# A graph-network kernel: the search for edge blocks runs alone, and sixteen groups of keys and values can wait for positions instead of eleven

## The chip, the cores and the metric

The kernel runs on one core of one Trainium2 chip. The metric is device time in microseconds (us) of one launch, the median of three runs. The profile is one more execution, with its own time. The engines are TensorE (PE, and PEld for its weight loads), VectorE (DVE), ScalarE (ACT), GpSimd (POOL) and SyncE (SP), which here only issues DMAs.

## The reference, cut to what matters

6250 nodes with 128 features, 200000 edges sorted by destination, 16 node types, 32 edge types, 8 heads of 16. `typed_linear` multiplies each node by the matrix of its own type. Two such layers run one after the other, then a projection, a residual and a normalisation.

```python
k = typed_linear(x, ntype, Wk).reshape(n, H, HS)
q = typed_linear(x, ntype, Wq).reshape(n, H, HS)
v = typed_linear(x, ntype, Wv).reshape(n, H, HS)
kT = jnp.einsum('nhd,htdo->nhto', k, Watt)
vT = jnp.einsum('nhd,htdo->nhto', v, Wmsg)
kw = kT[src, :, etype]
m = vT[src, :, etype]
a = jnp.einsum('ehd,ehd->eh', kw, q[dst]) * pri[:, etype].T / SQRT_D
att = edge_softmax(a, dst, n)
msg = (m * att[:, :, None]).reshape(-1, H * HS)
hag = jax.ops.segment_sum(msg, dst, num_segments=n)
h = jax.nn.silu(typed_linear(hag, ntype, Wa))
```

## The kernel before

Nodes are cut into 49 tiles of 128 and, for the preparation, into 25 groups of two tiles (the last has one). The time has two parts: a preparation that ends when the table of the first layer stands in DRAM, and two layers whose work is gathering rows of such tables, one row for each of 128 edges at a time (L914, 1613 gathers a layer).

The preparation has three strands, which share the engines:

- **Typed products** (`first_typed`, `one_typed`, `typed`). For each group its rows are loaded and transposed; for each of 16 types DVE makes a masked copy `xm` (L427), and PE multiplies it by that type's key and value weights into one PSUM bank `kv` (L442, 32 products for a group, which run as two passes each). Four `xm` buffers are there, so mask t waits for the product of mask t-4. Then `kv` is copied to `kT` and `vT` (L451, L453), which have KEPT buffers each.
- **The search** (`prepare`). Where each node's edges begin is found in steps: the destinations are compared with the first of each of 512 blocks (POOL writes `cols` L527, DVE makes 40 `less` tiles at L532 in two buffers, PE counts them at L536); the block numbers `blk_i` (L542) index 50 gathers on POOL (L550, ten `part` tiles of five gathers, two buffers); DVE counts in each (L558, L560); the degrees order the nodes (`hot` L599, a scan at L618), which gives their positions (`place32` L508). Records of the nodes follow (L651 to L660), and later steps that only the layers need.
- **Tables** (`first_tables`, `table_rows`). They wait for positions, since each row carries its node's. For each tile 16 products (L475, as four groups of four that run side by side) go through five PSUM banks `tab`, are copied by ACT or DVE into four staging tiles `st` of half a tile each (L484), get the position column (L840, twice a tile), and are written out (L865, four DMAs of 1028 KB a tile).

The order of each engine's instructions is written by a planner: steps of the strands are started by rank and by the time that the planner expects their inputs, and each engine's queue then runs in that order. An instruction that waits holds up all behind it on its engine. Queues of PE, DVE and ACT thus interleave the three strands, and the real times decide who waits. `plan.run()` is called for the preparation twice: once up to the test whether the edges are sorted (here they are, so `sort_edges` is skipped at run time), and once for the rest; the layers have a plan of their own.

Of the kernel before, what the change touches and what calls it, by code (L numbers as in the profile page):

```python
# [31 lines left out]
F32 = mybir.dt.float32  # L32
# [6 lines left out]
P = 128  # L39
# [12 lines left out]
XM = 4  # L52
MARGIN = 8.0
AHEAD = 2
KEPT = 11
STAGES = 4
SPARE = 1.0
DRIFT = 15.0
# [150 lines left out]
def dve_us(n):  # L209
    return 0.15 + n / 960  # L210


def act_us(n):
    return 0.14 + n / 1200
# [18 lines left out]
def gnn_kernel(ctx: ExitStack, tc: tile.TileContext, x, src, dst, etype, ntype, Wk, Wq, Wv, Wa,  # L233
               Watt, Wmsg, pri, skip, ln_g, ln_b, ff_w, ff_b, out):
    nc = tc.nc
    N, D = x.shape
# [3 lines left out]
    NTILE = -(-N // P)  # L240
# [3 lines left out]
    EC = KB * BL  # L244
    EP = P * EC
# [21 lines left out]
    def dtile(name, shape, dt=F32):  # L267
        return dram.tile(shape, dt, tag=name, name=name)
# [9 lines left out]
    dsort = dtile("dsort", [NBLK, BL], I32)  # L278
    csort = dtile("csort", [NBLK + 1, BL], I32)

    def ctile(name, shape, dt=F32):
        return const.tile(shape, dt, tag=name, name=name)


    ident = ctile("ident", [P, P])
# [57 lines left out]
    edges, flagged = {}, When()  # L343
# [103 lines left out]
    def copied(pool, tag, acc, M, bufs, needs):  # L447
        us, e = yield ("ACT", "DVE"), (act_us(M), dve_us(M)), needs
        t = pool.tile([P, M], F32, tag=f"{tag}{M}", name=tag, bufs=bufs)
        if e == "ACT":  # L450
            nc.scalar.copy(t, acc[:, :M])  # L451
        else:
            nc.vector.tensor_copy(t, acc[:, :M])  # L453
        return t, us
# [36 lines left out]
    ps = early.enter_context(tc.tile_pool(name="ps", bufs=1, space=bass.MemoryType.PSUM))  # L491
    NC1 = NTILE + 1
    ov = ctile("ov", [P, NTILE, 2], I32)
    placed, known = When(), When()
    place32 = first.tile([P, NTILE], F32, tag="place32", name="place32")
    kinds_r = first.tile([P, RT], F32, tag="kinds_r", name="kinds_r")
    nc.gpsimd.iota(kinds_r, pattern=[[1, RT]], base=0, channel_multiplier=0, allow_small_or_imprecise_dtypes=True)
# [13 lines left out]
    def prepare():  # L511
        stage = ExitStack()
        sp = stage.enter_context(tc.tile_pool(name="search", bufs=2, side="right"))
# [9 lines left out]
        for t0 in range(0, NC1, CB):  # L523
            n = min(CB, NC1 - t0)
            us = yield "POOL", 1.5, ()
            cols = sp.tile([P, CB, P], F32, tag="cols", name="cols")
            nc.gpsimd.iota(cols, pattern=[[1, CB], [NTILE, P]], base=t0, channel_multiplier=0,  # L527
                           allow_small_or_imprecise_dtypes=True)
            for k in range(KB):
                us = yield "DVE", 0.5, [us]  # L530
# [3 lines left out]
                for t in range(n):  # L534
                    c = k * NC1 + t0 + t
                    nc.tensor.matmul(blk_ps[:, c : c + 1], less[:, t], ones_b[:, 0:1], start=True, stop=True)  # L536
        us = yield "DVE", 1.0, [got]
# [2 lines left out]
        nc.vector.tensor_scalar(blk, blk, -1.0, 0.0, op0=ALU.add, op1=ALU.max)  # L540
        blk_i = pp.tile([P, NC1], I32, tag="blk_i")
        nc.vector.tensor_copy(blk_i, blk)  # L542
        begin = pp.tile([P, NC1], F32, tag="begin")
        seen = [us]
        for t0 in range(0, NC1, CB):
            n = min(CB, NC1 - t0)
            us = yield "POOL", n * GATHER_US, [us, *seen[-2:][:1]]
# [24 lines left out]
        sp = stage.enter_context(tc.tile_pool(name="order", bufs=1, side="right"))  # L572
# [8 lines left out]
        us = yield "DVE", 0.6, ()  # L581
# [3 lines left out]
        us = yield "DVE", 0.2, ()  # L585
# [10 lines left out]
        BT = BINS * NTILE  # L596
# [4 lines left out]
        us = yield "DVE", 0.3, ()  # L601
# [3 lines left out]
        total = sp.tile([P, BT], F32, tag="total")  # L605
# [3 lines left out]
        for lhs, to in ((ones_b, total), (upper, ahead)):  # L609
            for c0 in range(0, BT, 448):  # L610
                us = yield "PE", Work(112), [counted]
                n_ps = tabs[c0 // 448 % len(tabs)]
                nc.tensor.matmul(n_ps[:, :448], lhs, hot_f[:, c0 : c0 + 448], start=True, stop=True)
                us = yield "ACT", act_us(448), [us]
                nc.scalar.copy(to[:, c0 : c0 + 448], n_ps[:, :448])
        yield "DVE", 2 * dve_us(BT), [us]
        upto = sp.tile([P, BT], F32, tag="upto")
        nc.vector.tensor_tensor_scan(upto, total, total, 0.0, op0=ALU.add, op1=ALU.max)  # L618
        yield "DVE", dve_us(BT), ()
        nc.vector.tensor_tensor(upto, upto, ahead, op=ALU.add)  # L620
# [2 lines left out]
        us = yield "DVE", dve_us(BT), ()  # L623
# [8 lines left out]
        us = yield "DVE", 1.0, ()  # L632
# [10 lines left out]
        us = yield "DVE", 1.0, ()  # L643
# [4 lines left out]
        for t in range(NTILE):  # L648
            us = yield "DVE", dve_us(P) + dve_us(4 * NTILE), spent[-3:][:1]
# [5 lines left out]
            us = yield "PE", Work(4 * NTILE), [us]  # L655
# [3 lines left out]
        us = yield "DVE", dve_us(4 * NTILE), [us]  # L659
# [5 lines left out]
        us = yield "DVE", 0.3, [us]  # L665
# [9 lines left out]
        for g in WIDE:  # L675
# [5 lines left out]
            for j, t in enumerate(g):  # L681
                us = yield "POOL", XG_US, ()
# [7 lines left out]
        for t in range(NTILE):  # L690
            span = slice(offset[t], offset[t] + profile[t])
            us = yield "POOL", GATHER_US, ()
# [16 lines left out]
        us = yield "DVE", 0.8, ()  # L709
# [4 lines left out]
        us = yield "PE", Work(P), [us]  # L714
# [9 lines left out]
        for g in WIDE:  # L724
            n = len(g)
            us = yield "DVE", dve_us(n * P), ()
# [3 lines left out]
            us = yield "PE", Work(n * 32), [us]  # L730
# [3 lines left out]
            us = yield "ACT", act_us(n * P), [us]  # L734
# [8 lines left out]
        us = yield "DVE", dve_us(NTILE * NT), ()  # L743
        nc.vector.tensor_tensor(one_of, ty[:, :, None].to_broadcast([P, NTILE, NT]),
                                kinds[:, None, :].to_broadcast([P, NTILE, NT]), op=ALU.is_equal)
        for i in range(L):
            us = yield "SP", 0.4, ()
            sk = sq.tile([P, NT], F32, tag="sk", name=f"sk{i}")
            nc.sync.dma_start(out=sk, in_=skip[i][None, :].to_broadcast([P, NT]))
            us = yield "DVE", 2 * dve_us(NTILE * NT), [us + 3.0]  # L750
# [3 lines left out]
            us = yield "ACT", 1.6, [us]  # L754
            nc.scalar.activation(alpha[i], alpha[i], AF.Exp, scale=-1.0)
            us = yield "DVE", 1.0, [us]
# [15 lines left out]
    sts = [first.tile([P, RT // 2, ROW + 1], F32, tag=f"st{c}", name=f"st{c}") for c in range(STAGES)]  # L772
# [5 lines left out]
    def bank(pool, name):  # L778
        return pool.tile([P, GT * P], F32, tag=name, name=name)

    tabs, kv, xb = [bank(ps, f"tab{i}") for i in range(5)], bank(ps, "kv"), bank(ps, "xb")

    def load_nodes(n0, n):
        t = ap.tile([P, GL, P], F32, tag="rows", name="rows", bufs=3)
        full = min(n, (N - n0) // P)
        if full < n:
            nc.vector.memset(t, 0.0)
        if full:
            nc.sync.dma_start(out=t[:, :full], in_=x[n0 : n0 + full * P].rearrange("(j p) d -> p j d", p=P))
        if full < n:  # L790
            left = N - n0 - full * P
            nc.sync.dma_start(out=t[:left, full], in_=x[n0 + full * P : N])
        return t
# [2 lines left out]

    def first_typed(part):
        for i in part:
            g = GROUPS[i]
            n0, n = g[0] * P, len(g)  # L800
            M = n * P
            got = yield "SP", 0.9, read[-3:][:1] if i > 2 else ()
            rows = load_nodes(n0, n)
            ti = ap.tile([P, HALF], I32, tag="types_i", name="types_i")
            valid = min(M, N - n0)
            if valid < M:
                nc.vector.memset(ti, -1)
            nc.sync.dma_start(out=ti[:, :valid], in_=ntype[n0 : n0 + valid][None, :].to_broadcast([P, valid]))
            plan.spawn(one_typed(i, rows, ti, got + 3.0), RANK["typed"])
            read.append(masked_at[i])  # L810

    masked_at = [When() for _ in GROUPS]
    def one_typed(i, rows, ti, got):
        g = GROUPS[i]
        n = len(g)
        M = n * P
        us = yield "DVE", dve_us(M), [got] + ([masked_at[i - 2]] if i > 1 else [])
        tf = ap.tile([P, HALF], F32, tag="types", name="types")
        nc.vector.tensor_copy(tf[:, :M], ti[:, :M])
        xT, us = yield from transposed(xb, rows, n, [got] + ([masked_at[i - 1]] if i else []))  # L820
        end, masked_at[i].us = yield from typed(
            ap, "xm", xT, tf, M, [(wk, kv[:, :HALF]), (wv, kv[:, HALF:])], [], [kv], (1,),
            made[i - 1] if i else 0.0, [us])
        if i >= KEPT:
            yield "SP", 0.0, [used[i - KEPT]]
        kT, ks = yield from copied(ap, "kT", kv[:, :HALF], M, KEPT, [end])
        vT, vs = yield from copied(ap, "vT", kv[:, HALF:], M, KEPT, [end])
        columns[i] = kT, vT
        made[i].us = max(ks, vs)
# [47 lines left out]
    with tc.manual_schedule():  # L877
        plan.spawn(first_typed(range(AHEAD)), RANK["typed"])
        plan.spawn(load_edges(), RANK["prepare"], 1.0)
        plan.spawn(relation_blocks(), RANK["late"], 25.0)  # L880
        plan.run()
    unsorted = nc.values_load(edges["flag"][0:1, 0:1], min_val=0, max_val=E)
    with tc.If(unsorted > 0):
        sort_edges(tc, ident, edges["dst_i"], edges["comb"], dsort, csort, EC, NTILE, N, EP, tabs)
        nc.sync.dma_start(out=edges["dst_i"], in_=dsort_rows)
    nc.vector.tensor_copy(bounds, edges["dst_i"].rearrange("p (k b) -> p k b", k=KB)[:, :, 0])
    prep.close()
# [1 line left out]
    with tc.manual_schedule():  # L889
        plan.spawn(first_typed(range(AHEAD, len(GROUPS))), RANK["typed"])  # L890
        plan.spawn(first_tables(range(len(GROUPS))), RANK["table"])
        plan.spawn(prepare(), RANK["prepare"], flagged.us + 6.0)
        plan.spawn(first_states(), RANK["late"])
        plan.run()
# [4 lines left out]
    tabs, ak, av = [bank(ps, f"tab{i}") for i in range(4)], bank(ps, "ak"), bank(ps, "av")  # L899
# [464 lines left out]
                plan.run()  # L1364


def sort_edges(tc, ident, dst_i, comb, dsort, csort, EC, NTILE, N, EP, banks):

    nc = tc.nc
    with tc.tile_pool(name="cnt", bufs=1, side="right") as cp:  # L1370
        psums = dict(t_ps=banks[0][:, :P], s_ps=banks[1][:, :NTILE], d_ps=banks[2][:, :P], n_ps=banks[3][:, :NTILE])

        def tl(name, cols, dt=F32):
            return cp.tile([P, cols], dt, tag=name, name=name)

        lanes = tl("lanes", P)
        nc.gpsimd.iota(lanes, pattern=[[1, P]], base=0, channel_multiplier=0,
                       allow_small_or_imprecise_dtypes=True)
        part = tl("part", 1)
        nc.gpsimd.iota(part, pattern=[[1, 1]], base=0, channel_multiplier=1,  # L1380
                       allow_small_or_imprecise_dtypes=True)
        lower = tl("lower", P)
        nc.vector.tensor_scalar(lower, lanes, part, None, op0=ALU.is_lt)
        upper = tl("upper", P)
# [110 lines left out]
```

## Time and profile before

| what | value |
|---|---|
| median of three runs | 5319.89 us (5318.32 to 5320.77) |
| the profiled execution, its own time | 5318.69 us |
| span, first to last instruction | 5316.9 us |
| preparation, up to the first layer's first gather | 865.51 us |
| busy: PE, DVE, ACT, POOL | 48%, 74%, 18%, 65% of the span |
| granted TensorE clock, mean | 0.690 of full |

The span is 1.8 us shorter than the execution's own time. The shares are means over stages with different limits: POOL gathers in the layers, while the preparation is a matter of PE, DVE and DMA. The rows further down cut the preparation into stages.

### The profile page before, as it was taken

Reading aid. Unit: us, or ns where it says so; the run is one execution under the profiler, and the core shown is the slowest. Engines: PE = TensorE matmul, PEld = TensorE weight load, DVE = VectorE, ACT = ScalarE, POOL = GpSimd, SP = SyncE. Lnnn points to the kernel's source line nnn. Section 1 sums busy time; section 2 is a strip of 40 time slices with the busy share of each in tenths; the row PEclk is TensorE's granted clock in tenths of the full one; section 3 lists DMA queues with packets and bytes.
Section 4 is the critical chain, followed back from the end, with each engine's and each line's share of the span. In section 5 each row is a group of like instructions: output and inputs, shape, how many; then the busy total and the mean of one; then the engine's idle time right before and its main releaser. Section 6 shows DMA issues by size and latency. Waiting matters only on the chain. (4 is left out here: it accounts for less than half of the span.)

```text
span 5316.9 us, 36038 instructions
## 1 busy us (share of the span) xinstructions
PE 2575.6 (48%) x8599; PEld 1371.0 (26%) x8599; DVE 3924.0 (74%) x5652; ACT 930.8 (18%) x1917; POOL 3451.2 (65%) x3446
## 2 busy tenths in 40 slices
PE   6799994036646665676668731213223321221113
PEld 5555452013223332333234510101101111110002
DVE  5766663688887887778888727777777777776777
ACT  0133441002212222222224310000000000000001
POOL 2214103677777777777777347777777777777775
PEclk8899996567866676667778865656656655655556
DMA  3399898336556556665667544333333333333332
GB/s 98 113 354 396 340 374 269 97 104 235 158 184 232 176 170 226 233 203 180 206 220 286 222 148 121 102 115 115 116 106 114 115 110 105 110 112 108 110 103 74
DMA packets 324030, 925.54 MB, mean 174 GB/s; under 512 B 83047, under 2 KB 170132, under 8 KB 286176
## 3 DMA queue, kind: packets, MB, share of 16 engines
q0 software_dynamic: 162752, 441.12, 28.2%
q1 hardware_dynamic: 161056, 482.05, 24.2%
q8 instruction: 68, 1.11, 0.1%
q14 instruction: 154, 1.26, 0.1%
HBM read 489.36 MB, written 433.57 MB: 174 GB/s over the span
## 5 line engine op out<-in xcount | busy, mean ns | idle before, releaser
L914 POOL DMA_INDIRECT ring<-table,idx_all x3226 | 3230.5, 1001 | 1421.0 <-issue 1079.5
L938 DVE TENSOR_TENSOR ring<-ring,sb 128x2048 f32<-128x2048 f32 (+13 forms) x261 | 453.9, 1739 | 664.8 <-DMA ring<-table,idx_all 646.6
L969 DVE TENSOR_REDUCE add<-ring 128x128 f32<-128x2048 f32 (+13 forms) x269 | 749.5, 2786 | 7.8
L484 ACT COPY st<-tab 128x512 f32<-128x512 f32 x1138 | 601.3, 597 | 574.0 <-PE tab L475 454.5
L1048 DVE SCALAR_TENSOR_TENSOR xm<-types,xb 128x512 f32<-128x512 f32 (+3 forms) x880 | 486.7, 589 | 93.5 <-PE av L1056 79.0
L475 PE MATMUL tab<-bv,vT 32*128 32x512 f32 x1568 | 429.5, 804 | 113.1 <-ACT st L484 108.5
L940 DVE TENSOR_REDUCE sb<-ring 128x128 f32<-128x2048 f32 (+13 forms) x269 | 472.9, 1758 | 6.8
L965 DVE TENSOR_TENSOR ring<-ring,sb 128x2048 f32<-128x2048 f32 (+13 forms) x269 | 469.5, 1745 | 0.0
L475 PE MATMUL tab<-bk,kT 32*128 32x512 f32 x1568 | 408.9, 788 | 71.9 <-ACT st L484 56.2
L1056 PE MATMUL tab<-xm,wq 128*128 128x512 f32 (+3 forms) x416 | 213.6, 680 | 465.3 <-DVE xm L1048 465.3
L484 DVE COPY st<-tab 128x512 f32<-128x512 f32 x430 | 280.1, 686 | 210.5 <-PE tab L475 167.7
L1056 PE MATMUL av<-xm,wa 128*128 128x512 f32 (+3 forms) x736 | 323.2, 599 | 203.1 <-DVE xm L1048 202.5
L1056 PE MATMUL av<-xm,wq 128*128 128x512 f32 (+3 forms) x544 | 239.4, 593 | 129.1 <-DVE xm L1048 127.2
L1210 ACT COPY sb<-qr 128x128 f32<-128x128 f32 x96 | 25.9, 270 | 1556.2 <-DVE sb L940 1391.9
L442 PE MATMUL kv<-xm,wk 128*128 128x256 f32 (+1 forms) x800 | 266.5, 417 | 38.8 <-DVE xm L427 38.6
L442 PE MATMUL kv<-xm,wv 128*128 128x256 f32 (+1 forms) x800 | 249.3, 395 | 0.0
L1056 PEld LDWEIGHTS av<-xm,wa 128*128 128x128 f32 x736 | 152.2, 223 | 371.4 <-DVE xm L1048 248.8
L1056 PEld LDWEIGHTS tab<-xm,wq 128*128 128x128 f32 x416 | 100.3, 268 | 567.2 <-DVE xm L1048 507.5
L1056 PE MATMUL ak<-xm,wk 128*128 128x512 f32 (+3 forms) x480 | 228.4, 560 | 33.3 <-DVE xm L1048 33.3
L475 PEld LDWEIGHTS tab<-bv,vT 32*128 32x128 f32 x1568 | 177.2, 223 | 259.9 <-ACT st L484 203.7
L1056 PE MATMUL av<-xm,wv 128*128 128x512 f32 (+3 forms) x480 | 221.7, 546 | 0.0
L475 PEld LDWEIGHTS tab<-bk,kT 32*128 32x128 f32 x1568 | 166.6, 220 | 197.1 <-ACT st L484 114.4
(211 smaller groups left out, 2833.1 us busy)
## 6 DMA issues: line engine op xcount, KB each, us to landing
table<-st SPq DMA_DIRECT2D x196, 1028.0 KB
table<-st SPq DMA_DIRECT2D x98, 2048.0 KB
ring<-table,idx_all POOLq DMA_INDIRECT x3226
state<-init SPq DMA_DIRECT2D x2, 3528.0 KB
state<-state SPq DMA_DIRECT2D x98, 72.0 KB
types<-tyrow SPq DMA_DIRECT2D x20, 256.0 KB
rows<-in_x_dram SPq DMA_DIRECT2D x24, 128.0 KB
types_i<-in_node_type_dram SPq DMA_DIRECT2D x24, 128.0 KB
```

The source lines that it names most:

```text
L442: nc.tensor.matmul(to, w[:, t], xm, start=False, stop=last_of)
L475: nc.tensor.matmul(tab, cT[here, nodes], blk[here, t0 : t0 + per].rearrange("p t o -> p (t o)"), start=True, stop=True)
L484: (nc.scalar.copy if e == "ACT" else nc.vector.tensor_copy)(to, tab.rearrange("p (t o) -> p t o", o=width))
L914: nc.gpsimd.indirect_dma_start(out=ring[:, place], out_offset=None, in_=tables[layer], in_offset=bass.IndirectOffsetOnAxis(ap=idx[:, s : s ...
L938: nc.vector.tensor_tensor(kk, kk, q[:, None, :].to_broadcast([P, m, P]), op=ALU.mult)
L940: nc.vector.tensor_reduce(sc[:, s0 : s0 + m], kk.rearrange("p s (h d) -> p s h d", h=H), axis=AX.X, op=ALU.add)
L965: nc.vector.tensor_tensor(vv.rearrange("p s (h d) -> p s h d", h=H), vv.rearrange("p s (h d) -> p s h d", h=H), sc[:, s0 : s0 + m, :, None ...
L969: nc.vector.tensor_reduce(add, vv.rearrange("p s c -> p c s"), axis=AX.X, op=ALU.add)
L1048: nc.vector.scalar_tensor_tensor(xm[:, :M], types[:, :M], float(t), xT[:, :M], op0=ALU.is_equal, op1=ALU.mult)
L1056: nc.tensor.matmul(to[:, :M], w[:, t], xm[:, :M], start=(t == 0), stop=(t == NT - 1))
L1210: nc.scalar.copy(q, rows[0][:, j])
```

## The change

Three things change. The typed products from group AHEAD = 2 on are planned only after the search's blocks are known (`searched`). KEPT is 16 instead of 11. To find room for five more `kT` and `vT` buffers, the scan is done in place (`upto` is `total`), and the tiles of the sort that isn't run here lie in a staging tile. The first line of `first_typed`'s loop is the one that moves instructions.

```diff
-KEPT = 11
+KEPT = 16
...
-    placed, known = When(), When()
+    placed, known, searched = When(), When(), When()
...
         nc.vector.tensor_copy(blk_i, blk)
+        searched.us = us
...
-        upto = sp.tile([P, BT], F32, tag="upto")
+        upto = total
...
     def first_typed(part):
         for i in part:
+            if i == AHEAD:
+                yield "SP", 0.0, [searched]
             g = GROUPS[i]
...
-        sort_edges(tc, ident, edges["dst_i"], edges["comb"], dsort, csort, EC, NTILE, N, EP, tabs)
+        sort_edges(tc, ident, edges["dst_i"], edges["comb"], dsort, csort, EC, NTILE, N, EP, tabs, sts[0])
...
         def tl(name, cols, dt=F32):
-            return cp.tile([P, cols], dt, tag=name, name=name)
+            if dt is not F32:
+                return cp.tile([P, cols], dt, tag=name, name=name)
+            if name not in parts:
+                c0 = sum(t.shape[-1] for t in parts.values())
+                parts[name] = flat[:, c0 : c0 + cols]
+            return parts[name]
```

**First place: DVE, from the first block comparison on.** Before, with `less` the comparisons, `xm` the masks of the typed products, and `pr`, `bk` weights that wait for a load:

```order
L520 MEMSET ones_b 128x128
L532 TENSOR_SCALAR less<-cols,bounds 128x640
L819 CAST types<-types_i 128x256
L532 TENSOR_SCALAR less<-cols,bounds 128x640
L329 TENSOR_SCALAR pr<-pr 128x32
L330 TENSOR_TENSOR bk<-bk,pr 128x1024
L453 COPY vT<-kv 128x256
L427 SCALAR_TENSOR_TENSOR xm<-types,xb 128x256 x16
L819 CAST types<-types_i 128x256
L532 TENSOR_SCALAR less<-cols,bounds 128x640
```

Now, at the same place:

```order
L520 MEMSET ones_b 128x128
L532 TENSOR_SCALAR less<-cols,bounds 128x640 x40
L539 TENSOR_REDUCE blk<-pb 128x50
L540 TENSOR_SCALAR blk<-blk 128x50
L542 CAST blk_i<-blk 128x50
```

The weights, the copy of the first group's values and the sixteen masks of the second group have moved behind the search; PE's queue has the second group's products behind all of L536 as well.

**Second place: DVE, from the block numbers to the counts.** Before (L558 and L560 are the count in one `part` tile):

```order
L542 CAST blk_i<-blk 128x50
L819 CAST types<-types_i 128x256
L453 COPY vT<-kv 128x256
L427 SCALAR_TENSOR_TENSOR xm<-types,xb 128x256 x12
L558 TENSOR_TENSOR lt<-part,nid 128x1955
L560 TENSOR_REDUCE begin<-lt 128x5
L427 SCALAR_TENSOR_TENSOR xm<-types,xb 128x256 x4
L558 TENSOR_TENSOR lt<-part,nid 128x1955
```

Now (the count has the lines L559 and L561):

```order
L330 TENSOR_TENSOR bk<-bk,pr 128x1024
L453 COPY vT<-kv 128x256
L427 SCALAR_TENSOR_TENSOR xm<-types,xb 128x256 x16
L822 CAST types<-types_i 128x256
L427 SCALAR_TENSOR_TENSOR xm<-types,xb 128x256
L453 COPY vT<-kv 128x256
L427 SCALAR_TENSOR_TENSOR xm<-types,xb 128x256 x4
L559 TENSOR_TENSOR lt<-part,nid 128x1955
L561 TENSOR_REDUCE begin<-lt 128x5
L427 SCALAR_TENSOR_TENSOR xm<-types,xb 128x256 x5
L559 TENSOR_TENSOR lt<-part,nid 128x1955
```

The first count now stands behind 21 masks and both groups' hand-overs, where it stood behind 12 masks.

**Third place: PE, where one group's typed products end and the next begin, late in the tables.** Before, at tables of the sixteenth group (`vT_3423` and `kT_3413` are an older group's copies):

```order
L475 MATMUL tab4_124<-bk_246,kT_3413 128x512
L414 MATMUL xb_126<-ident_72,rows_4031 128x128 x2
L475 MATMUL tab0_120<-bv_256,vT_3423 128x512
L475 MATMUL tab1_121<-bv_256,vT_3423 128x512
L475 MATMUL tab2_122<-bv_256,vT_3423 128x512
L475 MATMUL tab3_123<-bv_256,vT_3423 128x512
L436 LDWEIGHTS zeros_104
L436 MATMUL kv_125<-zeros_104 128x512
```

Now, at tables of the twentieth (`kT_4707` is the copy of the `kv` that the first row here finishes):

```order
L442 MATMUL kv_125<-xm_4671,wv_99 128x256
L414 MATMUL xb_126<-ident_72,rows_4391 128x128 x2
L475 MATMUL tab3_123<-bk_246,kT_4707 128x512
L475 MATMUL tab4_124<-bk_246,kT_4707 128x512
L475 MATMUL tab0_120<-bk_246,kT_4707 128x512
L475 MATMUL tab1_121<-bk_246,kT_4707 128x512
L436 LDWEIGHTS zeros_104
L436 MATMUL kv_125<-zeros_104 128x512
```

The table products now use keys whose copy was only just asked for. Counted over PE's whole queue: when the first table product stands, 7.25 groups of typed products stand ahead of it before and 5.81 now; the last typed product stands behind 41.25 tiles of tables before and 47 now. In the layers the rows of every engine are the same in both.

## Rows read from the trace of the kernel before

**Rows 1.** Stages: length; busy PE, PEld, DVE, ACT, POOL; clock, DMA shares; GB/s.
```profile
39.00:102.00 63.00, 42.68 (x330) 33.55 (x329) 36.70 (x82) 0.75 (x2) 6.93 (x11) 0.79 0.12 17
102.00:187.00 85.00, 57.84 (x211) 45.07 (x209) 63.30 (x79) 2.04 (x6) 62.60 (x53) 0.82 0.47 128
346.00:375.00 29.00, 16.15 (x61) 8.88 (x60) 8.94 (x21) 4.70 (x9) 0.00 (x0) 0.71 1.08 369
375.00:470.00 95.00, 95.00 (x508) 55.07 (x506) 65.75 (x146) 36.40 (x68) 32.53 (x33) 1.00 1.02 406
566.00:642.00 76.00, 66.34 (x304) 34.17 (x303) 48.19 (x106) 30.72 (x61) 0.00 (x0) 0.91 0.74 298
642.00:766.00 124.00, 124.00 (x688) 73.45 (x687) 86.67 (x197) 48.02 (x90) 0.00 (x0) 1.00 0.90 367
766.00:837.00 71.00, 66.44 (x248) 36.96 (x240) 41.96 (x79) 35.69 (x62) 0.00 (x0) 0.66 1.00 414
```

**Rows 2.** The same for POOL's gathers of the first layer, L914.
```profile
866.00:3090.00 2224.00, 1615.13 (x1613) 0.71 0.59 196
```

**Rows 3.** Timeline, search: start, length, instruction, idle before and its releaser.
```profile
41.00 0.95 DVE L532 TENSOR_SCALAR less<-cols,bounds 128x640 bf16<-128x640 f32 x1 [0.75 <-POOL cols L527]
...
51.90 0.18 DVE L329 TENSOR_SCALAR pr<-pr 128x32 f32<-128x32 f32 x1 [9.29 <-DMA pr<-in_L_gnn_pri_dram]
...
70.83 0.55 DVE L532 TENSOR_SCALAR less<-cols,bounds 128x640 bf16<-128x640 f32 x1 [3.03 <-PE pb L536]
...
95.98 3.75 DVE L532 TENSOR_SCALAR less<-cols,bounds 128x640 bf16<-128x640 f32 x7 [0.25 <-PE pb L536]
...
102.51 1.18 POOL L550 DMA_INDIRECT part<-dsort,blk_i  x1 [5.96 <-DVE types L819]
```

**Rows 4.** Timeline of DVE and POOL: the first count, eleventh gather, `hot`.
```profile
113.95 2.19 DVE L558 TENSOR_TENSOR lt<-part,nid 128x1955 bf16<-128x1955 int32 x1
...
117.31 1.00 POOL L550 DMA_INDIRECT part<-dsort,blk_i  x1 [0.30 <-issue]
...
187.07 3.43 DVE L599 TENSOR_TENSOR hot<-bin__1343,bins 128x3136 bf16<-128x3136 f32 x1
```

**Rows 5.** Timeline of PE and ACT: typed products of the second group.
```profile
54.11 1.17 PE L442 MATMUL kv<-xm,wk 128*128 128x256 f32 x2
...
59.52 0.59 PE L442 MATMUL kv<-xm,wv 128*128 128x256 f32 x2
...
70.51 0.37 ACT L451 COPY kT<-kv 128x256 f32<-128x256 f32 x1 [30.77 <-PE kv L442]
```

**Rows 6.** Timeline of PE: the first four table products and the record product behind them.
```profile
233.22 1.14 PE L475 MATMUL tab<-bk,kT 32*128 32x512 f32 x8
234.29 0.60 PE L657 MATMUL pb<-what,here 128*128 128x196 f32 x2
234.72 0.59 PE L442 MATMUL kv<-xm,wk 128*128 128x256 f32 x2
```

**Rows 7.** Busy time by stage for the typed products alone, L442.
```profile
375.00:470.00 95.00, 57.97 (x235) 42.02 (x233) 1.00 1.02 406
...
642.00:766.00 124.00, 73.84 (x330) 55.35 (x328) 1.00 0.90 367
```

**Rows 8.** Busy time by stage for the table products alone, L475.
```profile
375.00:470.00 95.00, 39.55 (x264) 12.43 (x264) 1.00 1.02 406
...
642.00:766.00 124.00, 52.85 (x344) 17.12 (x345) 1.00 0.90 367
```

**Rows 9.** Timeline: last tiles, next weights, the first layer's gather.
```profile
824.53 0.37 DVE L840 TENSOR_SCALAR st<-kinds_r,place 128x16 f32<-128x16 f32 x2
...
834.57 0.37 DVE L840 TENSOR_SCALAR st<-kinds_r,place 128x16 f32<-128x16 f32 x2
...
853.80 0.77 SPq L308 DMA_DIRECT2D wq<-in_L_gnn_Wq_dram  x1
...
865.51 1.01 POOL L914 DMA_INDIRECT ring<-table,idx_all  x1 [303.35 <-DVE low L995]
```

More of the change, by code (lines that the diff above doesn't have):

```diff
@@ L1364, in gnn_kernel, with sort_edges @@
                 plan.run()
-def sort_edges(tc, ident, dst_i, comb, dsort, csort, EC, NTILE, N, EP, banks):
+def sort_edges(tc, ident, dst_i, comb, dsort, csort, EC, NTILE, N, EP, banks, room):
     nc = tc.nc
@@ L1371, in sort_edges @@
         psums = dict(t_ps=banks[0][:, :P], s_ps=banks[1][:, :NTILE], d_ps=banks[2][:, :P], n_ps=banks[3][:, :NTILE])
+        flat, parts = room.rearrange("p t c -> p (t c)"), {}
         def tl(name, cols, dt=F32):
-            return cp.tile([P, cols], dt, tag=name, name=name)
+            if dt is not F32:
[4 more added lines that the diff above has]
+            return parts[name]
         lanes = tl("lanes", P)
```

## The prediction

> **What bounds the kernel now.** I read the stages first. From 866 us on POOL issues one gather after another: 1613 of them fill 1615 of the 2224 us of the first layer [rows 2], and the order of instructions in both layers is untouched, so I take everything behind the first gather (5316.9 - 865.5 = 4451.4 us) as fixed. The change can only move the end of the preparation, 865.5 us.
>
> In the preparation the tables are the long piece. From 375 to 470 us and from 642 to 766 us PE is busy all the time at the full clock of 2.4 GHz, while DMA stands at a share of 1.02 and 0.90; from 766 us on only tables are left, PE's mean clock is 0.66 of full, and DMA sets the pace at a share of 1.00 [rows 1]. Two tiles that follow each other there are 834.57 - 824.53 = 10.0 us apart [rows 9]. So the tables have two limits close together: PE while typed products run beside them, DMA when they don't. They cannot start before positions are known, which is the end of the search's chain.
>
> In that chain the first place to look is the comparisons. The first runs at 41.00 us; DVE is then stuck until 51.90 us behind weights whose load is late, and the third comparison comes at 70.83 us, released by PE, whose queue had the second group's typed products in front. Where no masks stand between them, seven comparisons take 3.75 us, 0.54 each. The first block gather starts at 102.51 us [rows 3].
>
> **The change, step by step.**
>
> *The search alone.* 40 comparisons at 0.54 are 21.4 us. With the first as slow as it was (0.95, POOL writing beside it) and 1.4 us for the last count and the block numbers, the first gather is due at 41.0 + 0.4 + 21.4 + 1.4 = 64.2, say 64.4 us: 38 us earlier. The cover of this is nothing: the stretch from 39 to 102 us had PE busy for 42.7 us with work that is not removed, only put behind [rows 1]. If the comparisons cost what the mixed rows show, at most 0.95 each, the end would be 81; I take the pace of the seven, which is the same work without masks.
>
> *What is late next.* The first count now waits on DVE behind 21 masks (second place). After the block numbers, DVE does the cast, `pr`, `bk` and the copy of values, some 2 us, to 66; then the second group's products run. Before they took from 54.11 to the copy at 70.51, 16.4 us, the first passes 1.06 to 1.17 a pair and later ones 0.59 [rows 5], that is at 1.2 and then at 2.4 GHz. So they end near 83, and the count, which needs four or five more masks and the first product of the third group, starts near 86. POOL has two `part` buffers: its eleventh gather must wait for this count to have read the first (2.2 us), so it goes at 88.3, 23.9 us after the first gather. Before it went 117.31 - 102.51 = 14.8 us after [rows 4]. That gives back 9 us. The remaining 40 gathers and their counts are POOL's pace, as before: `hot` starts at 187.07 - 38.1 + 9.1 = 158.1 us, 29 us earlier. From `hot` to the first table product it was 233.22 - 187.07 = 46.1 us [rows 4, 6]; the steps between are the same and the in-place scan does the same work, so the first table product comes at 204.2. The bounds of this step: if the second group's products find the full clock, the count comes some 3 us sooner; if they stay at the lower one to the end, 32 products at some 0.85 instead of 0.43 put it 11 us later.
>
> The Trainium skill speaks against this step: "TensorE: Matmul & The Clock Gate" (Part 1) says that idleness throttles the array to half its clock and that activity releases it, and a search of one-column products is near idle. By that alone the second group would start slow, as it did before after a wait; the rows show that it recovered after some 5 us, so the sum keeps the 16.4 us, and the rule's worst case is the 11 us of the bound.
>
> *Sixteen buffers.* In PE's order typed products lead the tables by at most 5.81 groups now, where it was 7.25. A lead that small never asks for the twelfth buffer, let alone the sixteenth: no wait goes, none comes, 0 us.
>
> *PE's ledger from the first table product to the last typed one.* Four table products that run side by side take 234.29 - 233.22 = 1.07 us [rows 6], so a tile takes 4.28. A group of typed products is 64 passes and a tile of tables 32 passes: from 375 to 470 us there are 235 and 264, so (95 - 8.25 x 4.28) / 3.67 = 16.3 us a group; from 642 to 766 us 330 and 344, so (124 - 10.75 x 4.28) / 5.16 = 15.1 [rows 7, 8]. I take 15.7. Before: 25 - 7.25 = 17.75 groups and 41.25 tiles, 279 + 177 = 455 us, in the 533 us from 233 to 766. The other 78 us are the stall at 346 to 375 us, where PE was busy for 16 of 29 us at a DMA share of 1.08, the thin stretch at 566 to 642 us [rows 1], and 49 record products at 0.43 [rows 6], 21 us. All this work is still there; I keep 78. Now: 19.19 groups and 47 tiles, 301 + 201 = 502 us.
>
> *New idle time of PE.* The first ten tiles now have only 2.13 groups beside them: per tile 4.28 + 3.3, and with the records some 2.4, which is 10.0, as much as DMA needs for a tile [rows 9]. Two limits that are equal never overlap fully: 0 to 1.5 us a tile, I take 7 us in all. In the last nine groups each table product stands right behind the copy that it needs (third place). A copy is 0.37 us [rows 5]; bounds 0 and, if the copy queues behind two more of `tab`, some 2 us; I take 0.4, 4 us in all.
>
> *The sum.* 204.2 + 502 + 78 + 7 + 4 = 795 us for the last typed product, which was at 766. But then 7.75 tiles followed at DMA's pace, and now two: 8.6 us by PE, 20 by DMA; I take 14, so the last tile is numbered at 809 instead of 834.57. From there to the next weights' load it was 853.80 - 834.57 = 19.2 us [rows 9], with DMA behind; with less behind it 10 to 19, I take 16. That load comes at 825 instead of 853.8: 29 us less. The profiled execution, 5318.7, becomes 5290; the median lies 1.2 above it, so 5291.
>
> **The rivals.**
>
> *Handed back.* The 29 us of the chain are spent in the tables: a group costs 16.3 and not 15.7 (1.44 groups more, and 19.19 times 0.6: 11.5 us), and the second group's products stay at 1.2 GHz (11 us). Then 6 us are left: 5313. For it: PE is full in the rows already, and the work put behind was done under the search for nothing. Against it: the tail wasted PE for six tiles.
>
> *The stalls shrink.* The 78 us are not a law: 76 us at 566 to 642 had only 128 typed passes' worth of work, and with tables further ahead and fewer products at once the state writes may cost less. If 28 of the 78 go, it is 5263. Against it: DMA has 49 tiles of 10.0 us, so it can't end before 214 + 490 + 19 = 723 plus state writes and rows, some 40; 763 would be 90 us less, which bounds it.
>
> *Slower.* The hand-over in the third place: where the lead is one group, every table group waits for its `kT`, which ACT does in order behind copies that wait for a free staging tile, which waits for DMA. It decides from (29 + 10.6) / 9 = 4.4 us above my 0.4 for each of nine groups. At 6 us it would be 5291 + 9 x 5.6 = 5341. Against it: typed products of the same group stood between in the order, so that the last copies of `tab` are 1.9 us old when the key copy is asked for.
>
> *It doesn't do what it says.* The comparisons stay at the mixed pace since POOL and not PE held them; then the chain gains 20 instead of 38, and the end 11: 5308. I count it with the first rival.
>
> **How the numbers follow.** A measurement of this kernel tells some 0.2% (10.6 us) from no change. My forecast, 11 to 45 us less, 0.63. Stalls that shrink, 45 to 70 less, 0.13. Handed back, within 10.6 us, 0.18. Slower 0.06. Faster is then 0.76. The range takes in the bounds of the chain (-3, +11), of a group's price (15.1 to 16.3, 12 us each way) and of the tail (10 us each way), and reaches into the two neighbours: 5262 to 5318. The likeliest case's own is 5274 to 5308.
>
> **What the profile will show.** First gather near 64, eleventh 24 us behind it, `hot` near 158, first table product near 204. Ten tiles in the first 127 us of tables; the last typed product near 795; two or three tiles behind it; next weights near 825. Wrong would be: a first gather after 75, an eleventh gather without the pause, PE idle before table products whose `kT` is being copied, or a first layer whose length differs.

## The result, and the profile after

| | before | after |
|---|---|---|
| median of four runs each | 5320.33 us (5318.32 to 5321.04) | 5290.03 us (5288.56 to 5291.53) |
| the profiled execution, its own time | 5318.69 | 5290.87 |
| its span | 5316.9 | 5289.1 |
| the first layer's first gather | 865.51 | 836.64 |
| from there to the end of the span | 4451.4 | 4452.5 |

The ratio is 0.9944, with an interval of 0.9932 to 0.9957: 30 us faster, where 5291 us was forecast. In the profile the preparation ends 28.9 us earlier, and the layers have the length that they had.

The timeline of after shows the steps. They answer to [rows 3] (first comparison, first block gather), [rows 5] (copy of the second group's keys), [rows 4] (first count, eleventh gather, `hot`), [rows 6] (first table product) and [rows 9] (last tiles, next weights, first gather of the layers). Columns are as there.

```profile
40.48 23.39 DVE L532 TENSOR_SCALAR less<-cols,bounds 128x640 bf16<-128x640 f32 x40 [0.74 <-POOL cols L527]
...
65.36 1.18 POOL L551 DMA_INDIRECT part<-dsort,blk_i  x1 [4.69 <-DVE types L822]
...
83.62 0.37 ACT L451 COPY kT<-kv 128x256 f32<-128x256 f32 x1 [44.40 <-PE kv L442]
...
86.26 2.19 DVE L559 TENSOR_TENSOR lt<-part,nid 128x1955 bf16<-128x1955 int32 x1
...
88.72 1.00 POOL L551 DMA_INDIRECT part<-dsort,blk_i  x1 [10.44 <-DVE lt L559]
...
159.73 3.42 DVE L600 TENSOR_TENSOR hot<-bin__1197,bins 128x3136 bf16<-128x3136 f32 x1
...
207.88 1.14 PE L475 MATMUL tab<-bk,kT 32*128 32x512 f32 x8
...
345.26 1.57 ACT L484 COPY st<-tab 128x512 f32<-128x512 f32 x3 [23.56 <-DMA table<-st]
...
794.78 0.27 ACT L451 COPY kT<-kv 128x128 f32<-128x128 f32 x1 [0.92 <-PE kv L442]
...
806.26 0.37 DVE L843 TENSOR_SCALAR st<-kinds_r,place 128x16 f32<-128x16 f32 x2
...
824.54 0.77 SPq L308 DMA_DIRECT2D wq<-in_L_gnn_Wq_dram  x1
...
836.64 1.01 POOL L917 DMA_INDIRECT ring<-table,idx_all  x1 [295.62 <-DVE low L998]
```

One row now holds all 40 comparisons. `hot` comes 27 us earlier, the first table product 25, the next weights 29. The stages of after, columns as in [rows 1]:

```profile
39.00:65.00 26.00, 11.62 (x201) 8.35 (x201) 24.23 (x45) 0.22 (x1) 9.23 (x11) 0.60 0.22 24
...
208.00:307.00 99.00, 98.89 (x538) 55.21 (x541) 84.33 (x216) 45.26 (x86) 5.85 (x7) 1.00 0.91 374
307.00:366.00 59.00, 39.51 (x190) 22.83 (x190) 25.88 (x59) 14.07 (x27) 4.66 (x6) 0.83 1.03 355
366.00:462.00 96.00, 95.52 (x496) 56.00 (x497) 65.05 (x144) 35.90 (x67) 33.48 (x34) 1.00 1.02 403
...
560.00:631.00 71.00, 65.61 (x315) 36.30 (x314) 46.07 (x101) 31.28 (x62) 0.00 (x0) 0.95 0.77 307
631.00:795.00 164.00, 162.19 (x905) 97.28 (x908) 111.26 (x253) 63.17 (x120) 0.00 (x0) 1.00 0.87 349
795.00:808.00 13.00, 12.02 (x64) 6.66 (x56) 11.05 (x21) 9.34 (x17) 0.00 (x0) 1.00 1.02 419
```

In the search PE has a mean clock of 0.60 of full and is busy for 11.62 of 26 us. From 208 to 794 us it is idle for 32.2 us, and 19.5 of them lie in the stretch around the state writes (307 to 366). And the stretch in which tables are alone at DMA's pace, 71 us in [rows 1], has shrunk to 13. The layers, read as in [rows 2], hold the same 1613 gathers in a window of the same length:

```profile
837.00:3061.00 2224.00, 1613.69 (x1613) 0.71 0.59 195
```

### The profile page after: what moved, and what is told of

Read it like the earlier page. It is cut to its first block, busy times and chain, and to the rows that moved or that the text cites. A ratio compares the mean times of both kernels' runs of the same rounds, so it can differ in the third digit from the quotient of the medians.

```text
span 5289.1 us, 36056 instructions
## 1 busy us (share of the span) xinstructions
PE 2550.8 (48%) x8591; PEld 1346.7 (25%) x8599; DVE 3921.5 (74%) x5650; ACT 930.1 (18%) x1919; POOL 3451.4 (65%) x3446
## 5 line engine op out<-in xcount | busy, mean ns | idle before, releaser
L475 PE MATMUL tab<-bv,vT 32*128 32x512 f32 x1568 | 393.7, 771 | 114.1 <-ACT st L484 110.0
L475 PE MATMUL tab<-bk,kT 32*128 32x512 f32 x1568 | 384.0, 768 | 70.5 <-ACT st L484 54.5
L442 PE MATMUL kv<-xm,wk 128*128 128x256 f32 (+1 forms) x800 | 262.1, 411 | 45.7 <-DVE xm L427 45.3
L442 PE MATMUL kv<-xm,wv 128*128 128x256 f32 (+1 forms) x800 | 244.3, 388 | 0.0
L475 PEld LDWEIGHTS tab<-bv,vT 32*128 32x128 f32 x1568 | 162.0, 215 | 253.6 <-ACT st L484 195.6
L475 PEld LDWEIGHTS tab<-bk,kT 32*128 32x128 f32 x1568 | 156.1, 214 | 188.4 <-ACT st L484 109.5
```

The lines of the kernel that those rows point to most:

```text
L442: nc.tensor.matmul(to, w[:, t], xm, start=False, stop=last_of)
L475: nc.tensor.matmul(tab, cT[here, nodes], blk[here, t0 : t0 + per].rearrange("p t o -> p (t o)"), start=True, stop=True)
```

## The experiments

Twelve runs of seven kernels. Beside the first eight (the first set: kept11, parts4, states_early, after_counts and each of these `_again`) the kernel before takes 6466 to 6469 us, beside the last four (the second set) 5322 to 5326, as above. The first set ran on chips 2 and 8 and the second on chips 2 and 11, so the number of the chip doesn't tell them apart, and what does isn't known. In the first set the trace of kept11 agrees with that of after up to some 460 us (first count 86.47, `hot` 159.74) and then shows waits for "remote", of which before and after have none (last section). For that set I go by marks, that is by the start times of the instructions listed above, and compare with kept11, which has the order of after row for row. A ratio is always to runs of the kernel before on the same chip.

**The buffers alone, from both sides** (kept11, kept11_again, kept16_only).

```diff
 # kept11: after with
-KEPT = 16
+KEPT = 11
 # kept16_only: after with
-            if i == AHEAD:
-                yield "SP", 0.0, [searched]
```

> The changed kernel with eleven buffers for keys and values instead of sixteen; the order of every engine's instructions is the same. My theory: the whole gain is the search, and the twelfth to sixteenth buffers are never asked for, since typed products lead the tables by 5.8 groups at most: 5290 us, within 2 of the changed kernel, first block gather at 65, first table product near 208, next weights near 825. Rival (the buffers carry part of the gain, because ACT or DVE would wait for an old buffer to be read): a wait of the kT and vT copies for PE appears and the time lies between 5295 and 5320.

> The same kernel as in kept11, because that run's chip was one on which the kernel before took 6469 us and engines waited for 'remote', which the trace of before never shows. My theory (the order of the changed kernel with eleven buffers is the changed kernel): 29 to 30 us below the kernel before, 5290 where that takes 5320. Rival (the five buffers carry part): 5295 to 5320, with waits of the kT and vT copies.

> The kernel before with sixteen buffers and all that makes room for them, without the wait for the search: the order of instructions is that of before. My theory (buffers, in-place scan and shared tiles are worth nothing): ratio 1.000 within 0.002, first block gather near 102.5, hot near 187, first table product near 233, next weights 29 us behind those of kept11 on the same chip. Rival (the buffers carry part of the gain): ratio 0.997 or less.

Measured: kept11 has 0.9965 (0.9940 to 0.9990) and again 0.9949 (0.9931 to 0.9967), where after had 0.9944; its first gather is at 65.30, its first table product at 206.56. The copies of keys and values wait as in after (ACT's for PE's products, 150.3 us in 20 waits beside 148.4 in 19), and none for an older buffer's reader. kept16_only has 0.9994 (0.9985 to 1.0003), a median of 5317.62 against 5321.88; its first table product is at 232.83. Its first gather and its next weights:

```profile
102.40 1.19 POOL L551 DMA_INDIRECT part<-dsort,blk_i  x1 [6.72 <-DVE types L820]
...
852.41 0.77 SPq L308 DMA_DIRECT2D wq<-in_L_gnn_Wq_dram  x1
```

All three are within 1.4 us of before. So sixteen buffers, the in-place scan and the shared room are worth nothing that can be measured; the wait for the search is the change. It moves two things out of the search's way at once, the weights whose load is late and the second group's masks and products [rows 3]. No run moves one without the other, so how much each is worth stays open.

**The pause before the eleventh gather** (parts4, parts4_again, parts3).

```diff
 # after with KEPT = 11, and bufs=4 (parts4) or bufs=3 (parts3)
-            part = sp.tile([P, CB, BL], I32, tag="part", name="part")
+            part = sp.tile([P, CB, BL], I32, tag="part", name="part", bufs=4)
```

> The changed kernel with eleven buffers of keys and values, and four part buffers for the block gathers instead of two; the order of instructions is the same, only POOL's eleventh gather no longer waits for the first count. My theory (the pause of 10.4 us before the eleventh gather is what was given back, and the chain up to the positions sets when tables start, so what the chain gains the end gains): no idle time before the eleventh gather, 1.8 to 2.3 us between gathers' starts at most, hot at 149 to 152 instead of 159.7, first table product 8 to 10 us earlier, 5281 us (5279 to 5284). Rival A (counts and masks on DVE, not gathers, set the pace behind the first count): hot at 156 to 160, 5287 to 5290. Rival B (the tables are held by PE's sum of work and an earlier start is handed back): hot near 150, but next weights still at 822 to 825, 5288 to 5290.

> The same kernel as in parts4. There the eleventh gather had no pause, but three waits of DVE's masks for 'remote', 3.1 to 3.8 us each, put the first count from 86.5 to 97.7 us, and hot came at 158.5. Two theories now. If that delay belonged to that chip: first count at 86 to 87, hot at 149 to 152, 5280 to 5284 us. If gathers that run on beside the second group's products delay them on any chip: first count at 94 to 98, hot at 157 to 159, 5288 to 5290.

> The changed kernel with eleven buffers of keys and values and three part buffers; the order of instructions is the same. POOL may issue 15 gathers before it waits for the first count, where four buffers let it issue 20 and the second group's products then stood still behind masks that waited for 'remote'. Theory A (that halt needs the longer unbroken run of gathers): first count at 86 to 88, hot at 152 to 156, next weights 4 to 7 us before those of kept11 (875.4 and 876.6 where it ran). Theory B (any gathers beyond the tenth hold up the second group's products there): first count at 90 to 98, hot at 157 to 160, weights at 874 to 877. The time itself can hardly tell 5 us.

parts4 has 0.9955 (0.9935 to 0.9976) and again 0.9958 (0.9942 to 0.9973), no better than kept11; weights at 875.52 and 875.19, where kept11 has 875.43 and 876.60. The pause before the eleventh gather went (one of 8.54 us came before the twenty-first), but in these runs another wait came. The timeline of parts4, DVE, at the end of the second group's masks:

```profile
82.06 0.42 DVE L427 SCALAR_TENSOR_TENSOR xm<-types,xb 128x256 f32<-128x256 f32 x1 [1.71 <-PE kv L442]
85.58 0.42 DVE L427 SCALAR_TENSOR_TENSOR xm<-types,xb 128x256 f32<-128x256 f32 x1 [3.11 <-remote]
89.78 0.42 DVE L427 SCALAR_TENSOR_TENSOR xm<-types,xb 128x256 f32<-128x256 f32 x1 [3.78 <-remote]
...
97.66 2.19 DVE L559 TENSOR_TENSOR lt<-part,nid 128x1955 bf16<-128x1955 int32 x1
```

POOL issued gathers without a break from 65.6 to 91.6 us, and the first count slid from 86.5 to 97.7 (97.2 in the second run), so that `hot` gained 1 to 3 us. None of the three theories of the first expectation had foreseen that. `hot`, at 158.47, does lie in rival A's range, but rival A has the time lost behind the first count, and here it is lost ahead of it. The second theory of the repeat describes it, for the first set. parts4 has no run in the second, so whether the halt belongs to the first set's conditions or to the run of 20 gathers stays open.

parts3, of the second set, has 0.9936 (0.9922 to 0.9949), 5285.60 us. Its timeline, from the first and sixteenth gather to the next weights:

```profile
65.44 1.18 POOL L551 DMA_INDIRECT part<-dsort,blk_i  x1 [4.70 <-DVE types L822]
...
88.93 1.00 POOL L551 DMA_INDIRECT part<-dsort,blk_i  x1 [4.06 <-DVE lt L559]
...
154.10 3.42 DVE L600 TENSOR_TENSOR hot<-bin__1197,bins 128x3136 bf16<-128x3136 f32 x1
...
818.46 0.77 SPq L308 DMA_DIRECT2D wq<-in_L_gnn_Wq_dram  x1
```

The pause is 4.06 instead of 10.44 us, 6.4 less; `hot` comes 5.6 us earlier than in after, the first table product (201.61) 6.3, the next weights 6.1. What the chain gains, the end gains, one to one. There is no halt behind these 15 gathers: the first count is at 86.47, as theory A has it. The intervals of the ratios of parts3 and after overlap, so that is read from the marks.

**The state writes** (states_early, states_early_again, both3).

```diff
 # states_early: after with; both3: also KEPT = 11 and part bufs=3
-            yield "SP", 5.5, [placed]
+            yield "SP", 5.5, [searched]
             nc.sync.dma_start(
                 out=state.rearrange("(t p) c -> p t c", p=P),
```

In the traces the rows of PE, DVE, ACT and POOL stand in the order of after, by line and tile name; on SP the two writes move ahead of the rows of the groups that are loaded after the search.

> The changed kernel with the two state writes (7 MB) issued when the block numbers are known instead of behind the eleventh tile's tables. My theory (part of the 78 us of stalls is the state write, in which PE was busy for only 39.5 of 59 us while tables waited for DMA; DMA is at a share of 0.4 from 65 to 102 us, so it is free there): the wait of 23.6 us at 345 goes, the first count stays at 86 to 88, and of PE's 19.5 idle us some 17 come back: 5273 us (5269 to 5277). Rival A (DMA's total sets the tables, not when it writes): the wait comes back as shorter ones, 5287 to 5291. Rival B (the writes get in the way of the block gathers and of rows for the typed products): first count or hot 10 to 18 us later, 5275 to 5290.

> The same kernel as in states_early. There the tables from 309 to 366 us kept PE busy for 56.6 of 57 us, and the next weights came 19.9 us earlier than in kept11, with hot 1.7 us later. My theory: the same 18 to 20 us here, 5271 us (5269 to 5274). Rival (with DMA fast, the lead is lost to DMA-paced tables further on, which the other chip's waits had hidden): 5275 to 5290.

> states_early with eleven buffers of keys and values and three part buffers. If the two gains add (state writes 20 to 23 us, a shorter pause 4 to 7), next weights come 25 to 30 us before those of kept11 on the same chip, at 846 to 851 if kept11's are 876, and the ratio is 0.990. If the state writes, which run from 65.6 to 81 us, hold up the extra gathers, weights at 852 to 857 as in states_early.

states_early has 0.9907 (0.9886 to 0.9929) and again 0.9905 (0.9882 to 0.9928), and its next weights come at 855.56 and 853.08, 19.9 and 23.5 us before those of kept11. both3 has 0.9892 (0.9877 to 0.9907), 5263.19 us: 59 us below the kernel before beside it, the best of all. Its stage of the former stall, and its next weights:

```profile
302.00:360.00 58.00, 57.68 (x307) 33.76 (x309) 41.33 (x92) 22.93 (x43) 11.71 (x12) 1.00 1.02 411
```

```profile
66.00 15.50 SPq L874 DMA_DIRECT2D state<-init  x2
...
797.95 0.77 SPq L308 DMA_DIRECT2D wq<-in_L_gnn_Wq_dram  x1
```

PE is busy for 57.68 of 58 us where it was for 39.51 of 59. The weights come 20.5 us before those of parts3 and 26.6 before those of after, so the two gains add. `hot` is at 154.41, 0.3 us behind parts3, and the first count at 86.78 instead of 86.47: the writes, now at 66 us, hold the chain up by next to nothing.

**The ledger, pushed the other way** (after_counts, three times).

```diff
-        searched.us = us
...
         yield "DVE", 0.0, [landed]
         yield from wait
+        searched.us = seen[-1]
         yield "DVE", 0.3, ()
```

> The changed kernel with the typed products from the third group on planned after the last count of the search instead of after the block numbers. In PE's order 3.25 groups of typed products stand ahead of the first table product instead of 5.81; the last typed product stands behind 47 tiles as before. My theory (from the first table product to the last typed one it is PE's ledger: 15.7 us a typed group, 4.28 a tile, 85 to 89 us besides): the first table product within 5 us of the changed kernel's 208, then 2.56 groups more beside the tables, so the last typed product at 830 to 836 instead of 795, 5325 to 5331 us. Rival (the tables are held by DMA at 10 us a tile, and typed products fit beside them): the last typed product moves by under 15 us, 5290 to 5305.

> The same kernel as in after_counts. There the first table product came at 200.0 us, 6.6 earlier than in kept11, and the next weights 22.9 us later. My theory (ledger of 15.7 us for each of 2.56 groups, less 7 to 8 us of the chain): last typed product at 825 to 830, 5320 to 5326 us. Rival (part of the typed work fits beside DMA-paced tables, as the other chip had it): 5308 to 5316.

> The same kernel as in after_counts, once more, for a chip on which the kernel before takes 5320 us. On the other chip the first table product came 6.6 and 9.3 us earlier than in kept11 and the next weights 22.9 and 20.2 us later, where the ledger (15.7 us for each of 2.56 groups that move beside the tables, less the chain's gain) asks for 31 to 34. My theory: with no halts for 'remote' it is the ledger, next weights at 850 to 859 instead of 824.5, 5315 to 5324 us, ratio 0.9990 to 1.0008. Rival (about 10 of the 40 us are hidden, since DMA and not PE holds some of the stretches): weights at 841 to 849, 5306 to 5314 us, ratio 0.9970 to 0.9988.

The ratios are 0.9981 (0.9956 to 1.0006), 0.9979 (0.9959 to 0.9999) and 0.9984 (0.9975 to 0.9993). In the third the first table product comes 8.3 us before that of after, the last tile is numbered at 827 us, and the next weights come 21.1 later:

```profile
199.54 1.14 PE L475 MATMUL tab<-bk,kT 32*128 32x512 f32 x8
...
845.60 0.78 SPq L308 DMA_DIRECT2D wq<-in_L_gnn_Wq_dram  x1
```

My 850 to 859 was wrong, and the rival's 841 to 849 holds; that the time, 5319.27, falls into my range is no support, since the kernel before took 5326.47 beside it, and the ratio is in the rival's range. So 2.56 groups beside the tables cost 29 us and not 40. Where the other 11 are, the windows from the first table product to the last typed one show. Of before, of after and of after_counts_third in this order, each for all instructions, then for L442 alone, then for L475 alone:

```profile
233.00:766.00 533.00, 507.44 (x2620) 293.75 (x2619) 368.31 (x932) 203.18 (x387) 100.61 (x100) 0.97 0.91 356
...
233.00:766.00 533.00, 283.50 (x1136) 205.68 (x1136) 0.97 0.91 356
...
233.00:766.00 533.00, 215.21 (x1328) 68.94 (x1329) 0.97 0.91 356
```

```profile
208.00:794.00 586.00, 553.83 (x2879) 318.08 (x2888) 405.06 (x1010) 230.04 (x438) 99.64 (x100) 0.97 0.93 364
...
208.00:794.00 586.00, 304.44 (x1223) 220.89 (x1224) 0.97 0.93 364
...
208.00:794.00 586.00, 241.29 (x1504) 77.73 (x1504) 0.97 0.93 364
```

```profile
200.00:815.00 615.00, 584.82 (x3058) 344.18 (x3058) 425.97 (x1065) 230.29 (x436) 99.64 (x100) 0.97 0.89 349
...
200.00:815.00 615.00, 345.47 (x1392) 252.57 (x1392) 0.97 0.89 349
...
200.00:815.00 615.00, 231.79 (x1504) 70.45 (x1496) 0.97 0.89 349
```

Divided by the groups and tiles that the order has in each window, a typed group costs 283.50 / 17.75 = 16.0, 304.44 / 19.19 = 15.9 and 345.47 / 21.75 = 15.9 us: a constant. A tile costs 215.21 / 41.25 = 5.2, 241.29 / 47 = 5.1 and 231.79 / 47 = 4.9: less where more typed work stands beside it. That is 9.5 of the 11 us. PE's idle time is 25.6, 32.2 and 30.2 us, 2 less than in after; the wait at the state writes was 16.6 us there instead of 23.6. The ends of products are modelled, so the split is no more exact than they are; and the busy times of lines overlap (next section). Counted without overlap the tiles still take 9.2 us less.

## Why the prediction was right, step by step

- **The search alone.** First block gather forecast at 64.4 us, measured 65.36. The 40 comparisons took 23.39 us, 0.58 each and not 0.54: the price came from seven rows of which one began beside a ramp of POOL's, and of the forty nine did (last section). Right, 1 us short.
- **The second group, and what is late next.** Copy of its keys forecast near 83, measured 83.62; first count 86 and 86.26; eleventh gather 88.3 and 88.72, with the pause that the forecast named; `hot` 158.1 and 159.73. Right. parts3 shows that the pause is what it was said to be, and that it costs the end about what it costs the chain.
- **The clock.** In after the passes of the second group take 1.06 us a pair from 68.43 us and 0.60 from 71.76, which are the 1.2 and 2.4 GHz of [rows 5]; PE had a mean clock of 0.60 of full in the search ahead of them.

```profile
68.43 1.06 PE L442 MATMUL kv<-xm,wv 128*128 128x256 f32 x2
...
71.76 0.60 PE L442 MATMUL kv<-xm,wv 128*128 128x256 f32 x2
```

  That agrees with the rule of "TensorE: Matmul & The Clock Gate" (Part 1) in the Trainium skill that was weighed there; the bound of 11 us, products slow to the end, did not come.
- **Sixteen buffers at 0 us.** Shown from both sides.
- **PE's ledger.** First table product forecast at 204.2, measured 207.88: 1.6 us from `hot`, and 2 more between `hot` and the tables (48.2 us, 46.1 in before). The in-place scan isn't the reason, since kept16_only has it and takes 46.3 there; the reason stays open. From the first table product to the last typed product's copy forecast 591 us, measured 587. The sum was right, its split was not: a tile was priced at 4.28 us, from the four products that ran first, and PE was busy for 5.1 on it. Part of that is counted twice, because in the profile a product begins before the one ahead of it has ended: L442, L475 and the record products (25.70 us) add to 571.43 us in after, where PE was busy for 553.83. If each moment is given to the product that began last, an estimate from the starts in the trace, a tile takes 4.9 us and a typed group 15.2. Over 47 tiles and 19.19 groups that is 28 us more than forecast and 10 less. In before it is as much, so these 18 to 20 us lay hidden in the 78 "besides" (of which the prediction names the parts of only 13 + 10 + 21 = 44) and did no harm to the sum. Nor is 4.28 wrong everywhere. Where typed products stand between a tile's own products, the next product starts 1.08 us after four of them:

```profile
640.75 1.14 PE L475 MATMUL tab<-bk,kT 32*128 32x512 f32 x8
641.83 0.70 PE L442 MATMUL kv<-xm,wk 128*128 128x256 f32 x2
```

  By the same estimate a tile takes 4.28 us from 631 to 794 us, as priced, and 5.8 from 462 to 560, with fewer typed products beside it. after_counts is where a ledger with one price for all stages missed, by 10 us.
- **New idle time.** 7 + 4 us were forecast; PE's idle time between the first table product and the last typed one grew from 25.6 to 32.2 us, 6.6. That the size is near is luck, for the place is another. The 7 us were to come in the first ten tiles, from two equal limits, and there PE is busy for 98.89 of 99 us. The 6.6 us came at the state writes: PE is idle for 19.5 of 59 us there, where it was for 12.9 of 29 in [rows 1]. Why that grew no run shows. In the other stages it rose by 4.2 us and fell by 4.3 (9.7 us from 566 to 642 us of before, 5.4 from 560 to 631 of after). The first stage of tables and the one ahead of that stretch, of before; for after see the stages at the top and the last section:

```profile
233.00:346.00 113.00, 113.00 (x620) 70.53 (x619) 87.28 (x229) 44.80 (x86) 8.16 (x9) 1.00 0.81 307
...
470.00:566.00 96.00, 92.94 (x453) 51.64 (x446) 71.48 (x238) 38.55 (x73) 59.92 (x59) 0.98 1.00 393
```

  The hand-over of the third place, on which the slower rival rested, costs next to nothing: PE is busy for 162.19 of the 164 us from 631 to 795, and those who waited for ACT's copies of keys in after (us, times) are

```profile
  PEld tab L475: 4.1, 8
  PE tab L475: 2.1, 8
```

  that is 0.26 us of PE for each of eight, where 0.4 for each of nine was forecast. The first ten tiles came 10.1 us apart, numbered from 216.7 to 307.4 us, where 10.0 and the 0.7 of two equal limits were forecast.
- **The tail.** Last tile forecast at 809, measured 806.26; from there to the weights 16 and 18.3; weights at 825 and 824.54. That the end is met within 1 us is luck in part: the steps were off by +3.7 (first table product), -3.9 (to the last typed product), -2.5 (to the last tile) and +2.3 us (to the weights), and these cancel.

Of the rivals, *handed back* does not hold, by the result and by parts3, *slower* by the stage above, and *it doesn't do what it says* by the one row of comparisons. *The stalls shrink* did not happen here: the stall at the state writes is still there, 23.56 us long, and PE is idle for longer in it. But it named the right place: states_early and both3 show that it is worth 20 us and goes when the writes move to a stretch in which DMA has room (its share was 0.37 from 65 to 102 us of after).

## What to carry to other kernels

Where a chain of small steps shares engine queues with bulk work that something else will wait for anyway, let the chain go first: the bulk work delays the chain by its place in the order, even where the engines have room. Then look for the next thing that the chain waits on (a buffer, here), and for bulk transfers that could run while DMA has room. In a ledger, a price holds for the stage that it is read from: by the estimate above a tile took 4.28 us of PE in one stage and 5.8 in another of the same kernel.

## What the runs showed of the hardware that was not expected

- **Runs in which the same program is a fifth slower.** Up to 460 us the trace of kept11 agrees within 1 to 2 us with that of after. Then, while POOL issues 49 small gathers (L694) one after another, the other engines wait for long. The longest waits of kept11 from 460 to 560 us (engine, line, what it waited for: us in total, times, longest):

```profile
ACT st L484 <- remote: 45.9, 3, 25.3
PEld tab L475 <- issue: 40.3, 17, 21.2
DVE xm L427 <- remote: 29.7, 3, 18.8
```

  The stage from 462 to 560 us, of kept11 and then of after:

```profile
462.00:560.00 98.00, 57.95 (x199) 28.70 (x198) 31.50 (x96) 17.91 (x35) 52.95 (x54) 0.70 0.53 190
```

```profile
462.00:560.00 98.00, 93.12 (x450) 51.32 (x451) 72.59 (x241) 40.58 (x79) 55.64 (x55) 0.97 0.99 391
```

  POOL does the same work in both; PE, DVE and DMA do about half. It costs some 50 us here (the first layer begins at 887.52), and from there to the end of the span it takes 6433.4 - 887.5 = 5546 us instead of 4452.5. From 560 to 880 us, where POOL is idle, no wait for "remote" is shown. What "remote" stands for the traces don't say; that it comes with POOL's unbroken issues was seen at two places (here and in parts4), but not tested, and such issues alone are not enough: behind the forty gathers that kept11 issues from 88.93 us on no wait for "remote" is shown, and in the second set none at all.
- **A comparison that begins while one of POOL's ramps runs takes longer, up to almost twice.** The comparisons of after (shortest, median and longest in ns):

```profile
L532 DVE TENSOR_SCALAR less<-cols,bounds x40: 532/553/1019, 40.5 to 63.3; 128x640 bf16<-128x640 f32 x40
```

  Eight of them begin while a `cols` runs and take 1.02 us, the first 0.95, and all others 0.53 to 0.55, also where a ramp begins while they run. Those eight `cols` take 0.97 us, where they take 0.68 in before (comparisons beside them 0.73 to 0.91). So the time of the others did not change, but the share of slow ones did: one in seven in the rows that the forecast used, nine in forty here. That is the 1 us by which the first gather missed.
- **Layers that differ by 8 to 10 us between runs of one order.** kept16_only's and after_counts_third's profiled executions have 4460 and 4463 us of layers, those of after, parts3 and both3 4452. Differences of that size between profiled executions are no sign of the preparation.
